# Neighbours' product with W_l made once per node: the mean layer of a graph network gathers products in place of rows

## The chip, the cores and the metric

The kernel runs as one program on one core of a Trainium2 chip. The metric is the device time of one execution in microseconds (us); of several runs the median is given. All arithmetic is float32 unless a type is named.

Names: PE is TensorE, which multiplies matrices; PEld are its weight loads; DVE is VectorE, ACT is ScalarE, POOL is GpSimd, which here issues the gathers and the scatter-adds (indirect DMAs); SP issues the plain DMAs. SBUF is the on-chip memory, PSUM the accumulators that PE writes.

## The reference

There are N = 3125 nodes with D = 512 features and E = 50000 edges (src, dst), sorted by dst. Four residual layers follow one another:

```
x = x + attention(layernorm(x))       # 8 heads, softmax over the edges into a node
x = x + ffn0(layernorm(x))            # 8 experts, each takes its best 256 nodes
x = x + mean(layernorm(x))            # below
x = x + ffn1(layernorm(x))            # 64 experts, 2 per node, and a shared dense part
...
def mean(x):                          # W_l, W_r: 512 x 512
    agg = segment_sum(x[src], dst)    # sum over the edges into a node
    h = (agg / max(deg, 1)) @ W_l + b + x @ W_r
    return h * sigmoid(h)
...
def ffn0(x):                          # expert e: W1[e] 512 x 128, W2[e] 128 x 512
    h = gelu(x[idx[e]] @ W1[e] + b1[e])
    out[idx[e]] += vals[e] * (h @ W2[e] + b2[e])
```

The sum over the edges and the product with W_l can change places: agg @ W_l = segment_sum((x @ W_l)[src], dst).

## The kernel before

Nodes are handled in NT = 25 tiles of 128 (the last has 53). The edges of a tile stand in 17 columns of 128 edges: 16 columns belong each to a quarter tile of 32 nodes (QCOLS = 4 columns for each of 4 quarters), and one column, gathered into the buffer sr, takes what does not fit. One gather (L121, an indirect DMA by POOL) brings one column: 128 rows of 512 features and a tail.

The stages follow one another. (1) A front prepares edge lists and the attention table. (2) The attention loop (gat_tiles) goes over the tiles: 17 gathers tgx a tile in groups of up to six columns; DVE weighs them (L882); PE adds them up per node by one-hot matrices (L899, messages). Beside it the class Rows makes, one tile later, what the first FFN needs: statistics and square root (stats, ACT L595), the normalised row (normal, stored to ec_table), its transposes in PSUM tile ec_tp (turn, copied by ACT L613), and router logits (logits, then take). Also beside it, the one-hot of the next tile is transposed (L826), copied by ACT (tohrt, L828) and multiplied into tpd (L836). (3) The class Choice finds each expert's 256 nodes by a serial chain of small DVE instructions and small PE sums. (4) The first FFN (expert_choice) goes over 8 experts: gather two halves of rows (ec_x), transposes, W1, GELU, W2, bias, gate, and a scatter-add into xd per half (L1266). The two halves name different rows and do not wait for each other; the next expert's wait for them. (5) Statistics of xd are computed and stored in its column D (the reciprocal deviation rs). (6) The mean and dense loop goes over the tiles as described next. (7) The experts' loop runs the 64 routed experts.

In stage 6 (second_half) edges(t) adds the 17 gathered columns, each weighed by the sender's rs, into a PSUM tile: first the column sr (L1823), then 32 matmul records for the 16 columns sx (L1829). DVE takes mean and variance of the sum (L1839 to L1841), ACT writes the mean row (L1843). PE transposes it (turned, L1849; ACT copies it out, L1851) and mean_layer multiplies: four products of mt with W_l and four of xt with W_r into one accumulator (product, L1859). DVE adds the bias (L1864), ACT applies SiLU (L1865), DVE adds the residual. The row is normalised; of it come the gate (L1877, read by DVE at L1381), the up products with two weights (read by ACT at L1884 and DVE at L1885) and the down product (DVE L1891).

The loop is software-pipelined by hand. PE's order in iteration i is: transposes of mean(i), xn2(i), xn3(i-1) and s(i-2); edges(i+1); mean_layer(i); gate(i-1); up(i-1); down(i-2). The instructions marked with pin stay in the written order on their engine. POOL's only work there is fetch(i+2): first sr, then 16 gathers into sx. sr has 2 buffers (se_r) and sx has 7 of four columns each (se_g), so a gather waits until the matmul that reads the older contents is done.

## Time and profile before

| what | time |
|---|---|
| median of 3 runs | 2334.58 us (2333.31 to 2347.64) |
| the profiled execution | 2344.47 us |
| its span | 2342.7 us, mean granted PE clock 0.833 |
| front | 0 to 196 us |
| attention loop | 196 to 850 us |
| choice of nodes | 850 to 945 us |
| first FFN | 945 to 1020 us |
| statistics | 1020 to 1050 us |
| mean and dense loop | 1050 to 1840 us |
| experts' loop | 1840 to 2342.7 us |

The limits of the stages are read from the timeline. The page's first part gives the busy time of each engine over the span:

```
PE 1639.1 (70%) x6698; PEld 804.5 (34%) x6698; DVE 1039.3 (44%) x2902; ACT 469.3 (20%) x876; POOL 1103.7 (47%) x1140
```

A row of the page's fifth part gives line, engine, operation, what is written and read with the shapes, the count; then the busy time of the group, the mean duration of one instruction in ns, and the idle time of that engine just before such an instruction, with what ended most of it. A float32 matmul stands in the records as more than one instruction: four products with a 512 x 512 weight are 8 records of 0.43 us at the full clock. An instruction that issues a DMA counts as busy only while it prepares it. "remote" as a releaser means that no event in the records names who ended the wait.

### The profile page before, as it was taken

The numbers are of one execution on the slowest core, as the hardware profiler recorded it, in microseconds if no ns is written. First come the engines' busy times: TensorE is split into PE (matmuls) and PEld (weight loads), VectorE is DVE, ScalarE is ACT, GpSimd is POOL, SyncE is SP. The second block draws the span as 40 slices with busy tenths as digits, with TensorE's granted clock in tenths as the row PEclk, the third lists the DMA queues.
The fourth block names the chain that finished last, engine by engine and source line by source line (L and its number), as shares of the span: only waits on it lengthen the run. The fifth ranks groups of instructions, "written<-read, shape, count | busy, mean of one in ns | idle before, by whom it ended". The sixth has DMA issues, their size and how long they took to land. (4 is left out here: it accounts for less than half of the span.)

```text
span 2342.7 us, 22566 instructions
## 1 busy us (share of the span) xinstructions
PE 1639.1 (70%) x6698; PEld 804.5 (34%) x6698; DVE 1039.3 (44%) x2902; ACT 469.3 (20%) x876; POOL 1103.7 (47%) x1140
## 2 busy tenths in 40 slices
PE   6683545554545532612799989989999899889986
PEld 3351222222222222400344444444444454445443
DVE  6354567666766757240233433433444422233221
ACT  1010112122222210100222222222223121112111
POOL 1404666666666600526555555555530245445443
PEclk9896666666766665855899999999999999999998
DMA  5115676776777653667666666666662499899981
GB/s 166 40 58 154 198 213 194 215 212 195 214 207 209 201 182 124 119 158 208 185 186 191 190 191 181 189 191 182 188 186 94 156 330 308 277 320 300 299 274 32
DMA packets 182468, 451.84 MB, mean 193 GB/s; under 512 B 48036, under 2 KB 51947, under 8 KB 182202
## 3 DMA queue, kind: packets, MB, share of 16 engines
q0 software_dynamic: 91840, 266.53, 42.1%
q1 hardware_dynamic: 79434, 182.03, 21.8%
q10 hardware_dynamic: 11056, 1.67, 0.4%
q8 instruction: 59, 0.97, 0.2%
q14 instruction: 79, 0.65, 0.1%
HBM read 399.52 MB, written 65.01 MB: 198 GB/s over the span
## 5 line engine op out<-in xcount | busy, mean ns | idle before, releaser
L121 POOL DMA_INDIRECT tgx<-gat_table,sidx x417 | 399.7, 958 | 220.4 <-issue 147.8
L121 POOL DMA_INDIRECT sx<-xd,sidx x392 | 372.0, 949 | 143.8 <-issue 113.6
L882 DVE TENSOR_TENSOR tgx<-tgx,aside 128x3072 f32<-128x3072 f32 (+2 forms) x74 | 233.5, 3157 | 58.9 <-ACT aside L876 45.6
L899 PE MATMUL tpm<-tgx,toh 128*32 128x256 f32 (+1 forms) x1568 | 200.4, 554 | 48.2 <-issue 38.6
L1859 PE MATMUL acc<-sh_w,x3t 128*128 128x512 f32 x400 | 177.1, 595 | 0.0
L1649 DVE TENSOR_TENSOR re_s<-re_s,re_ph 128x256 f32<-128x256 f32 x72 | 30.3, 421 | 267.0 <-ACT re_s L1648 263.8
L1646 PE MATMUL re_ph<-sx,re_xt 128*128 128x512 f32 x320 | 148.6, 608 | 0.0
L1653 POOL DMA_INDIRECT out<-re_y,re_both x32 | 50.3, 1572 | 181.2 <-DMA out<-re_y,re_others 151.4
L836 PE MATMUL tpd<-dpart,toht 128*128 128x192 bf16 x100 | 18.2, 329 | 158.3 <-ACT tohrt L828 138.3
L899 PEld LDWEIGHTS tpm<-tgx,toh 128*32 128x32 f32 x1568 | 68.5, 139 | 161.9 <-issue 125.8
L121 POOL DMA_INDIRECT re_x<-moe_table,node x64 | 64.7, 1011 | 120.1 <-DVE destf L1504 91.7
L1646 PE MATMUL re_ph<-w,re_xt 128*128 128x512 f32 x256 | 118.8, 608 | 0.0
L121 POOL DMA_INDIRECT sr<-xd,sidx x25 | 23.7, 947 | 191.1 <-PE acc L1823 156.8
L1829 PE MATMUL acc<-sx,qoh 128*32 128x512 f32 x784 | 97.0, 621 | 11.6 <-DVE qoh L1826 7.9
L1859 PEld LDWEIGHTS acc<-sh_w,x3t 128*128 128x128 f32 x400 | 74.2, 190 | 84.2 <-issue 84.2
L306 PE MATMUL pw<-gat_w,fr_xt 128*128 128x512 f32 x200 | 99.9, 647 | 1.7 <-issue 1.7
L1859 PE MATMUL acc<-sh_wl,mt 128*128 128x512 f32 x200 | 95.1, 619 | 2.9 <-issue 2.9
L899 PE MATMUL tpm<-tgx,tohr 128*128 128x256 f32 (+3 forms) x104 | 54.3, 637 | 54.3 <-issue 24.7
L1839 DVE BATCH_NORM_STATS2 e_st<-acc 128x6 f32<-128x512 f32 (+1 forms) x25 | 17.5, 699 | 167.3 <-PE acc L1829 121.1
L1859 PE MATMUL acc<-sh_w,sh_ht 128*128 128x512 f32 x200 | 90.2, 593 | 1.3 <-ACT sh_ht L1851 1.2
L1859 PE MATMUL acc<-sh_wr,xt 128*128 128x512 f32 x200 | 89.9, 592 | 0.0
L846 DVE TENSOR_REDUCE tdm<-tpd 128x128 f32<-128x384 f32 (+2 forms) x77 | 28.1, 421 | 126.8 <-PE tpd L838 87.7
(434 smaller groups left out, 2746.4 us busy)
## 6 DMA issues: line engine op xcount, KB each, us to landing
sx<-in_L_ffn_w SPq DMA_DIRECT2D x120, 512.0 KB
w<-in_L_ffn_w SPq DMA_DIRECT2D x64, 512.0 KB
wo<-in_L_ffn_w SPq DMA_DIRECT2D x32, 512.0 KB
tgx<-gat_table,sidx POOLq DMA_INDIRECT x417
gat_table<-row SPq DMA_DIRECT2D x24, 264.0 KB
xd<-xres SPq DMA_DIRECT2D x24, 264.0 KB
ec_table<-ec_row SPq DMA_DIRECT2D x24, 264.0 KB
sx<-xd,sidx POOLq DMA_INDIRECT x392
```

Of the source, the lines that this page charges most:

```text
L121: return nc.gpsimd.indirect_dma_start(out=out, out_offset=None, in_=table, in_offset=bass.IndirectOffsetOnAxis(ap=idx, axis=0),)
L306: pin(nc.tensor.matmul(pw, xts[t][:, k, :], w[:, k].rearrange("p h d -> p (h d)"), start=(k == 0), stop=(k == KD - 1)))
L836: pin(nc.tensor.matmul(pd[:, j // PDJ, j % PDJ * w:(j % PDJ + 1) * w], oht[:, j * P:(j + 1) * P], part4[:, t].rearrange("p i w -> p (i w)" ...
L846: pin(nc.vector.tensor_reduce(to, v.rearrange("p (c i h) -> p c h i", c=n, i=3), AX.X, OP.add))
L882: pin(nc.vector.tensor_mul(msg, msg, wgt[:, a:b, :, None].to_broadcast([P, g, H, DH])))
L899: pin(nc.tensor.matmul(pm[own, b, :cols.stop - cols.start], left, x[:, j, cols], **at))
L1646: self.pin(nc.tensor.matmul(ph, xt[:, k, :], w13[:, :, k, :], start=(k == 0), stop=(k == KD - 1)))
L1649: self.pin(nc.vector.tensor_mul(s, s, ph[:, 1]))
L1653: return self.nc.gpsimd.indirect_dma_start(out=self.out, out_offset=bass.IndirectOffsetOnAxis(ap=dest, axis=0), in_=y, in_offset=None, bou ...
L1829: pin(nc.tensor.matmul(pm[i * Q:(i + 1) * Q, :], oh[:, j, i, :], x[:, i, :D], start=False, stop=(j == QCOLS - 1)))
L1839: pin(nc.vector.bn_stats(st[:n], pm[:n]))
L1859: pin(nc.tensor.matmul(po, xt[:, i % KD, :], w[:, i % KD, :], start=(i == 0), stop=(i == n - 1)))
```

## The change

The attention loop makes V = xn @ W_l for each tile of nodes, from the transposes that the logits use already. ACT scales it back by the deviation (dev) and writes it to a buffer (given), and SP stores it to a new table vd. W_l is loaded early, and the mean of each of its columns is taken from it once (at t = 1), so that a row and the row less its mean give the same product. b2 W_l is formed once (t = 3 and 5).

Because the first FFN changes x after that, it adds its own share to vd: W2 W_l is formed per expert during the choice, as a list of 40 pieces (8 sets of four transposes, 32 products) of which a few are issued after each sum on PE (beside). Each expert then has two more products with W2 W_l, two more bias additions, and two more scatter-adds, into vd. The gate's scale moves from DVE to ACT.

The statistics store rs in vd's column D; xd loses its tail and its second half. In the mean loop the gathers read vd, so what is summed is already multiplied by W_l; the sum of edges goes straight into the accumulator of xn2 @ W_r. As xn2 is scaled by the degree first (rs2 multiplied by it), DVE multiplies the whole by 1/degree and adds the bias in one instruction. The mean's statistics, its row, its transposes and the product with W_l are gone. The loop is re-indexed: iteration i fetches for i+1 and sums the edges of i.

PE's order there becomes: transposes of xn2(i), xn3(i-1), s(i-2); xn2 @ W_r; the 16 columns sx; the column sr, which closes the sum; gate(i-1); up(i-1); down(i-2). sx has 8 buffers. The first three experts' weights are loaded in iteration 2 of this loop (before: beside the first FFN), the later five after the last mean layer.

```diff
--- before.py
+++ after.py
...
-EARLY, LATE = 3, 4
+EARLY, LATE = 3, 5
...
+        self.given = [sb.tile([P, XROW], F32, name=f"ec_given{i}", bufs=1) for i in range(2)]
...
-    def logits(self, t):
+        pin(nc.scalar.copy(self.xt, pt))
+    def logits(self, t, to):
+        self.lp = to
         for k in range(KD):
-            self.pin(self.nc.tensor.matmul(self.pt[:, 0, :X0], self.xt[:, k, :], self.wr[:, k, :],
+            self.pin(self.nc.tensor.matmul(to, self.xt[:, k, :], self.wr[:, k, :],
                                            start=(k == 0), stop=(k == KD - 1)))
+        self.pv = self.ps.tile([P, KD, P], F32, name="ec_tp").rearrange("p k w -> p (k w)")
+        for k in range(KD):
+            self.pin(self.nc.tensor.matmul(self.pv, self.xt[:, k, :], self.wl[:, k, :],
+                                           start=(k == 0), stop=(k == KD - 1)))
 
     def take(self, t):
-        self.pin(self.nc.vector.tensor_copy(self.lg[:, t, :], self.pt[:, 0, :X0]))
+        nc, pin = self.nc, self.pin
+        pin(nc.vector.tensor_copy(self.lg[:, t, :], self.lp))
+        v, n = self.given[t % 2], rows(t)
+        pin(nc.scalar.activation(v[:, :D], self.pv, AF.Copy, scale=self.dev.pop(t)))
+        nc.sync.dma_start(self.vd[t * P:t * P + n, :], v[:n])
+        if t == 1:
+            pc = self.ps.tile([P, KD, P], F32, name="ec_tp").rearrange("p k w -> p (k w)")
+            for k in range(KD):
+                pin(nc.tensor.matmul(pc, self.c["ones"], self.wl[:, k, :], start=(k == 0), stop=(k == KD - 1)))
+            pin(nc.vector.scalar_tensor_tensor(self.wl, pc[:, None, :].to_broadcast([P, KD, D]), -1.0 / D, self.wl,
+                                               op0=OP.mult, op1=OP.add))
+        if t == 3:
+            pb = self.ps.tile([P, KD, P], F32, name="ec_tp")
+            for k in range(KD):
+                pin(nc.tensor.transpose(pb[:, k, :X0], self.b2[:, k * P:(k + 1) * P], self.c["ident"][:X0, :X0]))
+            self.bt = self.sb.tile([P, KD, X0], F32, name="ec_bt", bufs=1)
+            pin(nc.vector.tensor_copy(self.bt, pb[:, :, :X0]))
+        if t == 5:
+            pb = self.ps.tile([P, KD, P], F32, name="ec_tp").rearrange("p k w -> p (k w)")
+            for k in range(KD):
+                pin(nc.tensor.matmul(pb[:X0], self.bt[:, k, :], self.wl[:, k, :], start=(k == 0), stop=(k == KD - 1)))
+            b = self.sb.tile([X0, D], F32, name="ec_bv", bufs=1)
+            pin(nc.vector.tensor_copy(b, pb[:X0]))
+            nc.sync.dma_start(self.b2d, b)
...
-                nodes.logits(t - 1)
+                nodes.logits(t - 1, logit)
...
+    def beside(self, n):
+        for _ in range(min(n, len(self.pieces))):
+            self.pieces.pop(0)()
...
             all_ = self.ps.tile([P, 3], F32, name="ch_ps")
             pin(nc.tensor.matmul(all_, self.k["same"], cnt, start=True, stop=True))
+            self.beside(1)
...
+            turned = {}
+            def turn2(e):
+                pt = ps.tile([P, KD, P], F32, name="w2_tp")
+                for i in range(KD):
+                    pin(nc.tensor.transpose(pt[:, i, :], w2[:, e, i * P:(i + 1) * P], c["ident"]))
+                turned[e] = ch.tile([P, KD, P], F32, name="w2_t", bufs=2)
+                pin(nc.scalar.copy(turned[e], pt))
+            def times_wl(e, i):
+                if i == 0:
+                    turned["to"] = ps.tile([P, D], F32, name="w2_ps")
+                to = turned["to"]
+                pin(nc.tensor.matmul(to, turned[e][:, i, :], wl[:, i, :], start=(i == 0), stop=(i == KD - 1)))
+                if i == KD - 1:
+                    pin(nc.scalar.copy(w2v[:, e], to))
+            pieces = [lambda: turn2(0)]
+            for e in range(X0):
+                if e + 1 < X0:
+                    pieces.append(lambda e=e: turn2(e + 1))
+                pieces += [lambda e=e, i=i: times_wl(e, i) for i in range(KD)]
+            choice = Choice(nc, pin, c, k, ch, ps, mine, pieces)
...
-                adds = []
+                for j, (w, b, to) in enumerate(((w2, b2t, xd), (w2v, b2v, vd))):
+                    adds = []
+                    for h in range(HALVES):
+                        py = ps.tile([P, D], F32, name=f"py{j}")
+                        pin(nc.tensor.matmul(py, ht[:, h * P:(h + 1) * P], w[:, e, :], start=True, stop=True))
+                        y = ys[j][(2 * e + h) % 4]
+                        pin(nc.vector.tensor_add(y[:, :D], py, b[:, e, :]))
+                        gate = x[e, h][:, D + e:D + e + 1]
+                        pin(nc.scalar.activation(y[:, :D], y[:, :D], AF.Copy, scale=gate))
+                        adds.append(nc.gpsimd.indirect_dma_start(
+                            out=to, out_offset=bass.IndirectOffsetOnAxis(ap=node[:, h * X0 + e:h * X0 + e + 1], axis=0),
+                            in_=y, in_offset=None, compute_op=OP.add,
+                        ))
+                    tc.declare_no_dep(adds[1].ins, adds[0].ins, reason="different rows of the table")
                 for h in range(HALVES):
-                    py = ps.tile([P, D], F32, name="py")
-                    pin(nc.tensor.matmul(py, ht[:, h * P:(h + 1) * P], w2[:, e, :], start=True, stop=True))
-                    y = ys[(2 * e + h) % 4]
-                    pin(nc.vector.tensor_add(y[:, :D], py, b2t[:, e, :]))
-                    gate = x.pop((e, h))[:, D + e:D + e + 1]
-                    pin(nc.vector.tensor_scalar(y[:, :D], y[:, :D], gate, None, op0=OP.mult))
-                    adds.append(nc.gpsimd.indirect_dma_start(
-                        out=xd[:N], out_offset=bass.IndirectOffsetOnAxis(ap=node[:, h * X0 + e:h * X0 + e + 1], axis=0),
-                        in_=y, in_offset=None, compute_op=OP.add,
-                    ))
-                tc.declare_no_dep(adds[1].ins, adds[0].ins, reason="different rows of the table")
+                    x.pop((e, h))
...
-                nc.scalar.dma_start(xd[g * P:(g + n) * P, D:D + 1].rearrange("(t p) o -> p t o", p=P), rs[:, :n, None])
+                nc.scalar.dma_start(vd[g * P:(g + n) * P, D:D + 1].rearrange("(t p) o -> p t o", p=P), rs[:, :n, None])
...
+        nc.vector.tensor_mul(rs2, rs2, rdeg[:, 1])
+        gp = ctx.enter_context(tc.tile_pool(name="se_g", bufs=8))
...
-                gather(nc, x[:, 0, :], xd[:N], sidx[:, c0:c0 + 1])
+                gather(nc, x[:, 0, :], vd, sidx[:, c0:c0 + 1])
                 xs = [x]
                 for j in range(QCOLS):
                     x = gp.tile([P, 4, XROW], F32, name="sx")
                     for i in range(m):
                         col = c0 + 1 + j * m + i
-                        gather(nc, x[:, i, :], xd[:N], sidx[:, col:col + 1])
+                        gather(nc, x[:, i, :], vd, sidx[:, col:col + 1])
                     xs.append(x)
...
-            def edges(t):
+            def edges(t, pm):
                 c0, m = tile_cols(t)[0], quarters(t)
                 oh, xs = state.pop(("oh", t)), state.pop(("sx", t))
-                pm = ps_a.tile([P, D], F32, name="acc")
                 ohr = wk.tile([P, P], F32, name="qohr", bufs=2)
                 pin(nc.vector.tensor_scalar(ohr, c["iota_f"][:, :P], sloc[:, c0:c0 + 1], xs[0][:, 0, D:D + 1],
                                             op0=OP.is_equal, op1=OP.mult))
-                pin(nc.tensor.matmul(pm[:m * Q], ohr[:, :m * Q], xs[0][:, 0, :D], start=True, stop=False))
                 for j in range(QCOLS):
-                    x = xs[1 + j]
                     pin(nc.vector.tensor_tensor(oh[:, j, :m], oh[:, j, :m],
-                                                x[:, :m, D:D + 1].to_broadcast([P, m, Q]), OP.mult))
+                                                xs[1 + j][:, :m, D:D + 1].to_broadcast([P, m, Q]), OP.mult))
                     for i in range(m):
-                        pin(nc.tensor.matmul(pm[i * Q:(i + 1) * Q, :], oh[:, j, i, :], x[:, i, :D],
-                                             start=False, stop=(j == QCOLS - 1)))
-                n = m
-                mean = wk.tile([P, D], F32, name="mean")
-                n = n * Q
-                if n < P:
-                    pin(nc.vector.memset(mean, 0.0))
-                st = wk.tile([P, 6], F32, name="e_st", bufs=2)
-                mv = wk.tile([P, 2], F32, name="e_mv", bufs=2)
-                shift = wk.tile([P, 1], F32, name="e_shift", bufs=2)
-                pin(nc.vector.bn_stats(st[:n], pm[:n]))
-                pin(nc.vector.bn_aggr(mv[:n], st[:n]))
-                pin(nc.vector.scalar_tensor_tensor(shift[:n], mv[:n, 0:1], -1.0, rdeg[:n, t:t + 1],
-                                                   op0=OP.mult, op1=OP.mult))
-                pin(nc.scalar.activation(mean[:n], pm[:n], AF.Identity, bias=shift[:n], scale=rdeg[:n, t:t + 1]))
-                state["mean", t] = mean
+                        pin(nc.tensor.matmul(pm[i * Q:(i + 1) * Q, :], oh[:, j, i, :], xs[1 + j][:, i, :D],
+                                             start=False, stop=False))
+                pin(nc.tensor.matmul(pm, ohr, xs[0][:, 0, :D], start=False, stop=True))
...
-            def mean_layer(t, mt, xt):
-                pw = product([(mt, wl), (xt, wr)])
-                pin(nc.vector.tensor_add(pw, pw, bias))
+            def mean_layer(t, xt):
+                pw = ps_a.tile([P, D], F32, name="acc")
+                for k in range(KD):
+                    pin(nc.tensor.matmul(pw, xt[:, k, :], wr[:, k, :], start=(k == 0), stop=False))
+                edges(t, pw)
+                pin(nc.vector.scalar_tensor_tensor(pw, pw, rdeg[:, 0, t:t + 1], bias, op0=OP.mult, op1=OP.add))
                 pin(nc.scalar.activation(pw, pw, AF.Silu))
...
             fetch(0)
             one_hot(0)
-            for i in range(-1, NT - 1):
+            load(1)
+            normal(0)
+            for i in range(NT - 1):
                 if i + 2 < NT:
                     load(i + 2)
-                    fetch(i + 2)
-                    one_hot(i + 2)
-                mt = xt = x3t = ht = None
-                if i >= 0:
-                    mt = turned(state.pop(("mean", i)), "mt")
-                    xt = turned(state.pop(("xn2", i)), "xt")
+                fetch(i + 1)
+                one_hot(i + 1)
+                if i == 2:
+                    early += [weights.load(e) for e in range(EARLY)]
+                x3t = ht = None
+                xt = turned(state.pop(("xn2", i)), "xt")
                 if i >= 1:
                     x3t = turned(state.pop(("xn3", i - 1)), "x3t")
                 if i >= 2:
                     ht = turned(state.pop(("s", i - 2)), "sh_ht")
-                edges(i + 1)
                 normal(i + 1)
                 chosen, pairs = todo.pop(("choose", i), None), todo.pop(("places", i), None)
                 if chosen:
                     chosen = router.choose(*chosen)
                 if pairs:
                     pairs = router.places(*pairs)
-                if i >= 0:
-                    mean_layer(i, mt, xt)
+                mean_layer(i, xt)
                 if i >= 1:
                     gate(i - 1, x3t)
                     up(i - 1, x3t)
...
-            weights.gp = gp
-            early += [weights.load(EARLY + k) for k in range(LATE)]
             t = NT - 1
             x, z = todo.pop(("choose", t))
             assert not todo and z == t - 1
-            mt = turned(state.pop(("mean", t)), "mt")
             xt = turned(state.pop(("xn2", t)), "xt")
             x3t = turned(state.pop(("xn3", t - 1)), "x3t")
             ht = turned(state.pop(("s", t - 2)), "sh_ht")
             first = router.choose(x, z)
-            mean_layer(t, mt, xt)
+            mean_layer(t, xt)
+            weights.gp = gp
+            early += [weights.load(EARLY + k) for k in range(LATE)]
```

## The prediction

> **What bounds the kernel now.** I read four views: the costliest groups of the page, the busy time cut at the stages, the timeline of one tile of the long loop, and the waits. The windows, cut at the ends of the attention loop (850), the choice (945), the first FFN (1020), the statistics (1050) and the loop over mean and dense layers (1840), say which engine could be the limit where; the columns are length, then busy time of PE, its weight loads, DVE, ACT, POOL, then granted clock, DMA share and GB/s:
>
> ```profile
> 196.00:850.00 654.00, 332.42 (x2122) 157.39 (x2122) 425.70 (x786) 136.83 (x297) 399.92 (x421) 0.66 0.69 200
> 850.00:945.00 95.00, 24.38 (x98) 19.43 (x99) 55.42 (x217) 4.31 (x6) 5.73 (x6) 0.50 0.53 181
> 945.00:1020.00 75.00, 41.82 (x147) 26.62 (x145) 18.64 (x32) 13.06 (x23) 35.48 (x26) 0.82 0.58 95
> 1050.00:1840.00 790.00, 662.17 (x2504) 301.25 (x2504) 300.70 (x973) 201.84 (x278) 396.16 (x419) 0.93 0.60 177
> ```
>
> The mean and dense loop is a third of the span, and PE is busy for 84% of it. That invites the reading "PE is the bound, take PE work away". The page's groups give the prices:
>
> ```profile
> L121 POOL DMA_INDIRECT tgx<-gat_table,sidx x417 | 399.7, 958 | 220.4 <-issue 147.8
> L121 POOL DMA_INDIRECT sr<-xd,sidx x25 | 23.7, 947 | 191.1 <-PE acc L1823 156.8
> L1859 PE MATMUL acc<-sh_wl,mt 128*128 128x512 f32 x200 | 95.1, 619 | 2.9 <-issue 2.9
> L1859 PE MATMUL acc<-sh_wr,xt 128*128 128x512 f32 x200 | 89.9, 592 | 0.0
> ```
>
> The second row is the one to stop at: POOL idles 157 us in front of the gather sr, because sr's two buffers come free by a matmul of the edges (L1823). So PE lets the stream of gathers start, once a tile. The timeline of one tile (start, length, what, in brackets the idle time before) shows what happens then:
>
> ```profile
> 1368.46 1.13 PE L1823 MATMUL acc<-sr,qohr 128*128 128x512 f32 x2 [0.55 <-DVE qohr L1821]
> 1369.52 3.64 PE L1829 MATMUL acc<-sx,qoh 128*32 128x512 f32 x32
> 1369.86 0.95 POOL L121 DMA_INDIRECT sr<-xd,sidx  x1 [7.42 <-PE acc L1823]
> 1371.11 0.94 POOL L121 DMA_INDIRECT sx<-xd,sidx  x1 [0.30 <-issue]
> ...
> 1380.06 1.00 PE L1877 MATMUL misc<-gt,x3t 128*128 128x64 f32 x8
> ...
> 1380.89 7.09 PE L1859 MATMUL acc<-sh_w,x3t 128*128 128x512 f32 x16
> ...
> 1387.82 3.60 PE L1859 MATMUL acc<-sh_w,sh_ht 128*128 128x512 f32 x8
> ...
> 1394.01 0.23 DVE L1381 COPY logit<-misc 128x64 f32<-128x64 f32 x1 [3.70 <-remote]
> 1394.11 0.60 ACT L1884 ACTIVATE sh_s<-acc 128x512 f32<-128x512 f32 x1 [4.18 <-remote]
> ...
> 1398.34 0.95 POOL L121 DMA_INDIRECT sr<-xd,sidx  x1 [7.54 <-PE acc L1823]
> ```
>
> The gate's matmuls (L1877) end at 1381.06, but their reader on DVE (L1381) starts at 1394.01. The first half of the up product ends at about 1384.5; its reader on ACT (L1884) starts at 1394.11. DVE and ACT had nothing left from 1390.3 and 1389.9. 17 gathers run from 1369.86 to 1390.79, one per 1.25 us, and their last bytes land at 1394.1 by the DMA records. In some 18 of the loop's tiles the same 13.0 and 9.6 us stand there. Completions that fall in the first 4 us of a stream are seen within 1 us (edges to L1839: 0.9), those with no gather in flight after 0.1. I read this as a rule of this trace: **deep in a stream of gathers, a product of PE is seen only when the stream has drained**. A tile is then stream 20.95, drain 3.2, and a chain of 4.3 to the next sr: 28.5 us. PE's 25 us fit inside; they are not what sets it. The waits of the attention loop look the same:
>
> ```profile
> ACT tohrt L828 <- remote: 168.1, 18, 14.5
> ```
>
> (sum, count, mean us of idle time.) That copy reads a transpose which had ended 9 us earlier where I looked (717.87 to 726.69), and restarts with POOL's next gather at 726.89.
>
> **The change, part by part.**
>
> *Mean loop, removed per tile:* four wl products (8 records, 3.7 us), four transposes and mt's copy, bn_stats, aggregate, shift on DVE (0.70, 0.18, 0.16) and the mean on ACT (0.78). PE falls from 25.3 to about 21.2 us (transposes 3 x 0.5, wr 3.6, edges 3.64, sr 1.1, gate 1.0, up 7.1, down 3.6), level with POOL's 17 gathers (21.3). None of this lies on the chain stream, drain, restart, so by itself it is worth nothing.
>
> *Moved:* edges now add into wr's accumulator. Order on PE before: mt, xt, x3t, ht transposes, sr's matmul, sx's 32, wl, wr. After: xt, x3t, ht transposes, wr, sx's 32, and sr's matmul last (it closes the sum). POOL's fetch still begins with sr and sr still has two buffers, so the stream that was let go by the first matmul of the edges is let go by the last, with wr ahead of it as well. The eighth sx buffer gives nothing, for sr stands ahead of it in the queue. With T0 the end of sr's matmul: stream from T0+0.35 to T0+21.3, drained at T0+24.5. After T0 PE has gate, up, down and the next xt and x3t transposes, 12.7 us, then ht's transposes, which need sh_s from the up product (ended at T0+4.6 and T0+8.1, so deep in the stream) and is held. From the drain: L1884 0.60, multiply 0.69, ht's transposes 0.66 with 0.2 of handing over, wr 3.6, sx matmuls 3.64, sr 1.1. Pitch = 24.5 + 10.5 = 35.0, against 28.5: **+6.5 per tile, 24 tiles, +156**.
>
> Here PE stands still from T0+12.7 to T0+26. The trace's row: in the attention loop, with such holes (9.1 us ahead of L836), the granted clock is 0.66, against 0.93 here with holes of 2.9. The Trainium skill ("TensorE: Matmul & The Clock Gate", section "What's actually happening") says that the array falls to half clock after an idle window of about 3.4 us and needs as long busy to come back. By the rule wr and the edges after each hole lose up to 3.4/2 to 3.4 us: +41 to +82. It speaks against the change, since less PE work makes longer holes. In the sum I leave it out, for half of the loop's matmuls here would still run back to back; the range has it.
>
> *Attention loop, added per tile:* V = xn W_l, 4 matmuls (8 records; 3.7 us at full clock, up to 7 at half), an ACT copy with a scale (0.6 to 0.8), a store of 264 KB; three one-off pieces (about 10 us in all, beside gathers). PE is busy 51% there, so the matmuls fit in. But ACT's copy of V waits for PE, and behind it in ACT's order stand the next tile's sqrt (L600, with a table load of 1.28) and tohrt's copy. If V is held to the drain as tohrt is, 0.7 + 1.3 + 0.3 = 2.3 us are put ahead of tohrt after it, and tpd, the reduce and the exponentials follow. Whether POOL's next stream waits for them: its buffers come free by earlier groups. Bounds 0 and +5 per tile (V at half clock ahead of group 0's messages besides), below nothing excluded, for nothing is taken away there. SP's tdst loads keep their place ahead of the new store. The nearest row is POOL's restart 0.2 us after tohrt, which is released at the same instant and not by it; I take +0.8 per tile: **+20** (0 to +120).
>
> *Choice:* 8 sets of transposes and 32 products of W2 with W_l in PE's gaps. At this stage's clock (0.50) about 1.3 and 1.75 each, 66 us; PE is idle for 70.6 of 95, so they just fit, in gaps that a serial DVE chain makes. Each can push a small matmul of that chain by at most 1.75, and some ten that remain at the end stand ahead of b1's transpose. **+8** (0 to +25).
>
> *First FFN:* two more products, adds and scatter-adds per expert. PE, DVE and ACT have room (42, 19, 13 of 75). POOL does not: a scatter-add is 1.59 us with 0.30 between. Per expert four of them and two gathers (0.98): 10.1 us, 81 for eight, with 11 of start and landing 92, against 75. Today's adds leave POOL waiting on each other's landing, which the new ones, to another table, can fill; that is in the 92. **+17** (0 to +35).
>
> *Other moves:* three experts' weights (4.5 MB) go from the first FFN's time to the third tile of the mean loop, where DMA is 60% busy, and the broadcast b2v adds 2 MB earlier: 0, covered by the DMA share; uncovered, some 5 us of drain in two tiles. The later sets are issued after the last mean layer: 0 (to +10); three sets are there. rs2 and deg: one small DVE multiply. Experts' loop: unchanged.
>
> Sum: 156 + 20 + 8 + 17 = +201. The profiled execution took 2344.5 (span 2342.7), 9.9 above the median of 2334.6, so on the median's scale 2535.
>
> **The rivals.**
>
> *Faster: completions are not what holds the tile.* If the late readers belong to before's order and the new one (few products between T0 and the stream's start) escapes, or the records mislead, the tile costs the larger of POOL's 21.3 and PE's 21.2 with today's 2.9 of waiting: 24.1, which is -4.4 x 24 = -106; with the +45 of the other stages -61: 2274. For it: the last tiles, without gathers in flight, run at 25 to 26.5, PE's own pace; wr is sometimes seen in time (L1864 3.1 us after its end). Against it: that 13.0 and 9.6 come back tile after tile, and in the attention loop too. It decides from the point where the up product's reader starts within about 4 us of its end.
>
> *Slower by the added work alone.* The held readers stay, but the chain after the drain is as short as now (wr running ahead before ht's transposes, or the stream starting with the edges): pitch 28.5 to 29.5, 0 to +24, with +45: 2370 to 2395.
>
> *The clock.* As forecast, with 3.4 us lost to half clock in each tile, or the attention loop at +5: 2535 + 60 or so, to 2600.
>
> **How the numbers follow.** Forecast (with its clock variant) 0.61, own range 2420 to 2600; added work alone 0.13; faster 0.26. About 1% is what a measurement here can tell from no change. Of the faster case 0.22 keeps more than 1% (it must lose no more than 38 us of its 61 to a dearer attention loop), 0.04 falls within 1%, with 0.02 more from a cheap version of the second rival; slower has the rest, 0.72. The range must take in half of the faster case to leave no more than 2 in 10 out: 2274 to 2600.
>
> **What would show it.** In the changed profile: idle time of sr on POOL (157) rises to 24 x about 13, or falls near nothing in the faster case; its releaser is the closing matmul of the edges; L1884's and the logit copy's counterparts start together at the drain; the windows of the loop show a clock well under 0.93 (forecast) or PE busy over 88% (faster). The attention loop's end is at 850 + 20, the first FFN has 32 scatter-adds and ends some 45 later. The forecast is wrong if the pitch of the mean loop is under 28.

## The result, and the profile after

The changed kernel takes 2485.1 us (median of 4 runs, 2479.1 to 2493.4), the kernel before beside it 2338.5: the ratio is 1.0625 (95% interval 1.0576 to 1.0674). It is slower by 6%. The profiled execution took 2479.1, its span is 2477.3.

Where the 134.6 us between the two profiled spans lie, with the stages cut at the same instructions in both (last message of the attention loop, first and last scatter-add, first matmul of the experts):

| stage | before | after | difference | forecast |
|---|---|---|---|---|
| to the end of the attention loop | 836.0 | 891.3 | +55.3 | +20 |
| choice of nodes | 113.8 | 133.9 | +20.1 | +8 |
| first FFN, its adds | 66.5 | 74.9 | +8.4 | +17 |
| statistics, mean and dense loop | 828.6 | 898.6 | +70.0 | +156 |
| experts | 497.8 | 478.6 | -19.2 | 0 |

The windows of the changed kernel, cut at its own stages (columns as in the prediction: attention loop, choice, first FFN, mean and dense loop):

```profile
196.00:891.00 695.00, 431.58 (x2302) 189.05 (x2302) 426.35 (x776) 148.39 (x316) 399.95 (x417) 0.73 0.66 195
891.00:1025.00 134.00, 91.03 (x252) 46.15 (x251) 60.30 (x232) 19.63 (x33) 5.98 (x10) 0.67 0.36 117
1025.00:1100.00 75.00, 49.49 (x163) 29.28 (x161) 20.83 (x32) 33.92 (x51) 60.20 (x42) 0.90 0.96 155
1165.00:1955.00 790.00, 561.20 (x2064) 250.38 (x2064) 243.54 (x759) 158.88 (x214) 375.77 (x396) 0.85 0.56 166
```

The last row ends with the last sums of edges; the prediction's window of before went on for 70 us behind them, so the two do not hold the same work. Over the whole stage (1100.1 to 1998.7 us, before 1016.3 to 1844.9) PE is busy for 607 us in place of 664, and the stage is 70 us longer: less work for PE did not make it shorter. The granted clock fell from 0.93 to 0.85 in the loop. The gathers of the mean loop before, which the prediction shows for sr alone, and then the groups of now:

```profile
L121 POOL DMA_INDIRECT sx<-xd,sidx x392 | 372.0, 949 | 143.8 <-issue 113.6
...
L121 POOL DMA_INDIRECT sx<-vd,sidx x392 | 372.1, 949 | 359.2 <-PE acc L1891 245.8
L121 POOL DMA_INDIRECT tgx<-gat_table,sidx x417 | 399.9, 959 | 266.0 <-issue 166.6
L1914 PE MATMUL acc<-sh_wr,xt 128*128 128x512 f32 x200 | 128.4, 801 | 0.8 <-issue 0.8
```

POOL's gathers are as long as before (949 and 959 ns). The idle time ahead of those into sx is now 359 us, and most of it ends with L1891, the sums of edges over sx; before, it was 144 us ahead of sx and 191 ahead of sr. It does not end with L1893, the closing matmul of sr. One tile of that loop, from the timeline:

```profile
1501.74 7.08 PE L1908 MATMUL acc<-sh_w,x3t 128*128 128x512 f32 x16
...
1505.79 0.60 ACT L1936 ACTIVATE sh_s<-acc 128x512 f32<-128x512 f32 x1
...
1508.66 3.60 PE L1908 MATMUL acc<-sh_w,sh_ht 128*128 128x512 f32 x8
...
1513.39 1.04 PE L1898 MATMUL tp<-ident,xn 128*128 128x128 f32 x8
...
1516.18 0.69 DVE L1943 TENSOR_TENSOR sh_o<-acc,x 128x512 f32<-128x512 f32 x1 [6.55 <-remote]
...
1517.82 0.95 POOL L121 DMA_INDIRECT sx<-vd,sidx  x1 [0.30 <-issue]
...
1521.88 0.59 ACT L1900 COPY xt<-tp 128x512 f32<-128x512 f32 x1 [15.50 <-remote]
...
1522.52 1.12 PE L1898 MATMUL tp<-ident,sh_s 128*128 128x128 f32 x4 [8.09 <-ACT xt L1900]
...
1523.43 4.83 PE L1914 MATMUL acc<-sh_wr,xt 128*128 128x512 f32 x8
...
1528.19 3.64 PE L1891 MATMUL acc<-sx,qoh 128*32 128x512 f32 x32
1529.64 0.94 POOL L121 DMA_INDIRECT sx<-vd,sidx  x1 [10.87 <-PE acc L1891]
```

The transposes of xn (L1898) end at 1514.43. ACT, which has nothing else to do, copies them at 1521.88; the last gather was issued at 1517.82 and its bytes landed at 1521.65. Then comes the chain: copy, ht's transposes (PE had stood still for 8.1 us), W_r, the sums, and POOL goes on at 1529.64 after 10.87 us. W_r takes 4.83 us here, 3.6 in the tiles of before: the clock has dropped in the hole (granted 1.00 from 1514.5 to 1519.0, 0.50 from 1519.1 to 1525.8, and 1.00 again from 1526.0).

### The profile page after: what moved, and what is told of

Same layout as the page of the kernel before. It is cut to its first block, busy times and chain, and to the rows that moved or that the text cites. A ratio compares the mean times of both kernels' runs of the same rounds, so it can differ in the third digit from the quotient of the medians.

```text
span 2477.3 us, 22626 instructions
## 1 busy us (share of the span) xinstructions
PE 1754.5 (71%) x6746; PEld 834.6 (34%) x6746; DVE 1020.8 (41%) x2829; ACT 485.4 (20%) x899; POOL 1128.7 (46%) x1157
## 5 line engine op out<-in xcount | busy, mean ns | idle before, releaser
L121 POOL DMA_INDIRECT sx<-vd,sidx x392 | 372.1, 949 | 359.2 <-PE acc L1891 245.8
L1718 PE MATMUL re_ph<-sx,re_xt 128*128 128x512 f32 x360 | 166.2, 605 | 0.0
L1891 PE MATMUL acc<-sx,qoh 128*32 128x512 f32 x784 | 110.5, 694 | 53.2 <-DVE qoh L1888 49.5
L1898 PE MATMUL tp<-ident,sh_s 128*128 128x128 f32 x100 | 25.4, 403 | 154.4 <-ACT xt L1900 135.9
L1914 PE MATMUL acc<-sh_wr,xt 128*128 128x512 f32 x200 | 128.4, 801 | 0.8 <-issue 0.8
L629 PE MATMUL ec_tp<-ec_wl,ec_xt 128*128 128x512 f32 x200 | 116.5, 733 | 1.2 <-issue 0.6
L883 DVE TENSOR_REDUCE tdm<-tpd 128x128 f32<-128x384 f32 (+2 forms) x77 | 28.1, 421 | 197.2 <-remote 72.6
L1916 DVE SCALAR_TENSOR_TENSOR acc<-acc,rdeg,sh_bias 128x512 f32<-128x512 f32 x25 | 19.0, 758 | 204.7 <-issue 97.7
L1718 PE MATMUL re_ph<-w,re_xt 128*128 128x512 f32 x216 | 99.8, 606 | 0.0
L1718 PEld LDWEIGHTS re_ph<-sx,re_xt 128*128 128x128 f32 x360 | 66.9, 196 | 67.3 <-issue 67.3
```

The lines of the kernel that those rows point to most:

```text
L121: return nc.gpsimd.indirect_dma_start(out=out, out_offset=None, in_=table, in_offset=bass.IndirectOffsetOnAxis(ap=idx, axis=0),)
L629: self.pin(self.nc.tensor.matmul(self.pv, self.xt[:, k, :], self.wl[:, k, :], start=(k == 0), stop=(k == KD - 1)))
L883: pin(nc.vector.tensor_reduce(to, v.rearrange("p (c i h) -> p c h i", c=n, i=3), AX.X, OP.add))
L1718: self.pin(nc.tensor.matmul(ph, xt[:, k, :], w13[:, :, k, :], start=(k == 0), stop=(k == KD - 1)))
L1891: pin(nc.tensor.matmul(pm[i * Q:(i + 1) * Q, :], oh[:, j, i, :], xs[1 + j][:, i, :D], start=False, stop=False))
L1914: pin(nc.tensor.matmul(pw, xt[:, k, :], wr[:, k, :], start=(k == 0), stop=False))
```

## The experiments

The experiments ran in later sessions than the first measurement, on three chips of one type (1, 4 and 11), and that turned out to matter. In each of these sessions the kernel before took 2126 to 2129 us, not 2335 to 2339. Which chip the first measurement ran on is not on record, so it is open whether the difference lies in the chip or in some condition of that session. Below they are called the first session and the later ones. Where an expectation speaks of a chip on which the kernel before takes 2335 us, it means the first session. Both kernels were run again unchanged, with a profile, beside experiments in one of the later sessions (chip 4).

**The two kernels again.**

> The kernel before, unchanged, for its profile beside the next three on the same chip. On the chip of the first four experiments the kernel before took 2129 us and not 2335. Theory (on that chip products are seen in time even deep in a stream of gathers, so the held chain is gone): where this run takes about 2130 us, the attention loop ends near 775 us and the distance of tiles in the mean loop is 25 to 26 us, PE's own pace; where it takes about 2335 us, the distance is 28.5 us and the readers of the gate and up products wait for the drain, as in the first profile.

> The changed kernel, unchanged, on the same chip. Theory for a chip where the kernel before takes 2130 us: the mean loop as in the run without products, 26 us a tile, attention and choice longer by some 9 and 19 us: 2195 to 2215 us, 3 to 4% slower than before. For a chip where the kernel before takes 2335 us: 2485 us as measured. Rival (the change costs the same everywhere): ratio 1.06 on both.

Measured: before 2127.3 in its profiled run (median of the runs beside it 2128.3), after 2204.9 (2200.5 to 2210.2), ratio 1.0345 (1.0296 to 1.0395). The windows of the attention loop and of the mean loop, the kernel before first:

```profile
196.00:719.00 523.00, 326.36 (x2072) 148.78 (x2072) 408.37 (x746) 136.08 (x285) 385.72 (x401) 0.68 0.81 238
...
941.00:1558.00 617.00, 582.14 (x2307) 262.97 (x2307) 260.14 (x803) 182.35 (x253) 392.70 (x413) 0.96 0.74 216
```

```profile
196.00:787.00 591.00, 403.43 (x2276) 179.06 (x2276) 413.13 (x750) 147.41 (x309) 383.30 (x401) 0.77 0.74 221
...
1063.00:1679.00 616.00, 536.75 (x2059) 233.04 (x2060) 244.86 (x758) 158.96 (x214) 379.81 (x396) 0.91 0.71 212
```

The attention loop of the kernel before ends at 718.7 (theory: 775) and its tiles are 21.6 us apart, 17 gathers of 1.25 us and nothing more; in the first session they were 25.4 apart. The mean loop's tiles are 25.5 us apart, and PE is busy for 94% of that loop. The readers of the transposes in the mean loop start within 0.1 us of the transposes or of the end of their engine's work, at any point of a stream. In the first session ACT's copy of xt started 3.3 to 8.8 us late in each of the 19 tiles of the changed kernel whose transposes ended 15 to 18 us into a stream. So the held readers (those that start late though their product is done and their engine is free) belong to the first session and not to the kernel. Here the change costs +68.6 in the attention loop, +15.7 in the choice, +11.1 in the FFN, -5.7 in the mean loop's stage and -9.6 in the experts. The waits of the changed kernel name two new causes (who waited for whom, then us in total, how often, the longest):

```profile
DVE tdm L883 <- PE tpd L625: 107.0, 23, 5.7
PEld acc L1891 <- DVE qoh L1888: 104.9, 37, 6.0
PE acc L1891 <- DVE qoh L1888: 77.8, 20, 5.2
POOL sx L121 <- PE acc L1891: 76.4, 16, 6.9
```

L883 are DVE's sums over tpd for the attention weights, L625 the router's logits, which the change moved into a free corner of tpd. L1888 scales the one-hots for the sums of edges.

**Sums of edges first.** The edit, in the mean loop (an excerpt, comments added):

```diff
...
+                edges(i)                 # starts the accumulator
                 xt = turned(state.pop(("xn2", i)), "xt")
...
                 mean_layer(i, xt)        # W_r closes it
+                prep(i + 1)              # DVE: qohr, qoh scaled by the deviation
...
```

> The sums of edges stand first in PE's order of each tile of the mean loop, ahead of the three sets of transposes; the product with W_r follows them and closes the sum; DVE's preparation of the one-hots is made one tile earlier. The work is the same. Theory (the tile is a stream of 17 gathers, its drain, and then the chain up to the first sums, which let the next stream go): nothing of the held chain is left ahead of the sums, so the distance of tiles falls from about 33 to 23 to 26 us, and the whole kernel from 2485 to 2270 to 2340 us. Rival (the loop is longer because PE, with longer holes, runs at a lower clock, or because the products in vd make the gathers slower): PE's and the gathers' work is unchanged, so 33 us and 2485 stay within 1%.

Measured 2130.2 us, ratio to before 1.0015 (1.0002 to 1.0028). Against the changed kernel's 1.0345 the gain is 75 us. The distance of tiles is 21.5 us, below what the theory said, since the gathers run without a break. No reader is held in that session, so it is not the held chain that this edit removed. It moves two things at once, PE's order and DVE's preparation; a later run tells them apart.

**W_r after the sums.** Only the order of the two in mean_layer is turned round; sr's matmul opens the sum.

> Only the product with W_r moves: after the transposes come the sums of edges and then W_r, in place of W_r and then the sums. Theory: the sums' start, which lets the stream go, comes earlier by the product's time, 3.6 to 4.8 us a tile, 24 tiles: 2485 falls by 85 to 115, to 2370 to 2400 us, and the idle time of POOL ahead of its gathers by as much. Rival (clock or gather speed): no change beyond 1%.

Measured 2265.3, ratio 1.065 (1.0621 to 1.0679): a miss, slower by 60 us than the changed kernel in a session of the same pace. The distance of tiles is 28.5, against 26.2. Here the sums wait for DVE's scaled one-hots, and W_r ahead of them filled part of that wait: PE's idle time ahead of the sums that ends with the one-hots is 124 us with W_r behind them, 78 with W_r ahead.

**Few gathers.**

```diff
...
-                    for i in range(m):
+                    for i in range(1):
...
                         gather(nc, x[:, i, :], vd, sidx[:, col:col + 1])
...
```

> Left out: three of every four gathers of the 16 columns in the mean loop; the sums read the gathered column four times, so PE, DVE and ACT work as before. 5 gathers in place of 17 make a stream of 6 us. Theory (products late in a stream are seen only when it has drained): no product is late any more, the distance of tiles falls to PE's own 21 to 23 us, the loop by some 240 us. Rival (the new order's chain or PE's clock sets the tile, and gathers only fill it): the distance stays above 29 us.

Measured: tiles 25.6 us apart, with 5 gathers, against 26.2 with 17, and not 21 to 23: the theory fails here, and the rival is right that the gathers only fill the tile (its 29 us was a figure of the first session). In every third tile it is 28 to 29 us, in the next 25 to 28, in the third 22.4, with or without the gathers. Something else in the new order sets them. Whether the loop of the first session would have become shorter was not tried.

**Without V and without the pieces.**

> Left out: the four matmuls of V in each tile of the attention loop (ACT scales the transposed row in V's place, the store to vd stays), and the 40 pieces that form W2 W_l beside the choice. Theory (V's matmuls come between the messages of a tile and what the next stream waits for): the attention loop ends at 836 to 845 us in place of 891, and the choice is 15 to 20 us shorter. Rival (it is the extra ACT copy ahead of the square root, or the stores, that cost): the attention loop still ends at 875 or later.

Measured (beside it the run with the sums of edges first, on the same chip, whose attention loop and choice are the changed kernel's): the loop ends at 777.9 against 786.6, the choice takes 115.8 against 135.1. So the pieces cost 19 us, as the theory said, but V's matmuls only 9, where the theory had some 50: there the rival holds. The stores and ACT's copy were still there, and so was the logits' place in tpd; the runs with the sums ahead of the logits, further down, tell these apart.

**W2 W_l in the loop of the first FFN, one expert ahead,** in place of the pieces, on top of the sums of edges first:

> The kernel with the sums of edges first, and W2 W_l of each expert formed in the loop of the first FFN, one expert ahead, in place of the 40 pieces beside the choice. Theory (the pieces make the choice about 19 us longer, since each stands ahead of a small matmul of the serial chain): the choice is 19 us shorter, the FFN at most 6 us longer, the whole 10 to 20 us below the same kernel with pieces (2130 us on the chip of the first four experiments). Rival (PE is as busy in the FFN as its adds allow): the FFN takes the 19 us instead.

Measured 2127.9, ratio to before 0.9993 (0.9975 to 1.0011), not distinguishable from the same kernel with pieces (1.0002 to 1.0028). Against the changed kernel in the same session the choice is 11 us shorter (123.2) and the FFN 7.5 longer (84.7): most of the time has moved and not gone, which is nearer to the rival.

**The sums over tpd ahead of the logits.** First on top of that kernel, then as the only edit of the changed kernel:

```diff
...
-            if t and a == col_groups(t)[-1][0]:
-                nodes.logits(t - 1, logit)
             if nxt and nxt[0] != t:
                 dm = collect(nxt[0])     # DVE: sums over tpd (comment added)
                 before, oh = pm, oh_next
+            if t and a == col_groups(t)[-1][0]:
+                nodes.logits(t - 1, logit)
...
```

> As the run before it, and in the attention loop DVE's sums over tpd for the next tile are issued ahead of the logits' matmuls, which since the change write a corner of the same PSUM tile. Theory (the sums wait for the logits only because both use tpd, 5.6 us a tile): the exponentials and the weighing start up to 5 us earlier in each tile, the attention loop's tile falls from 24.5 to 22 to 24 us, the whole by 10 to 50 us. Rival (the loop is set by the messages and the buffers): below 5 us.

> The changed kernel with one thing moved: in the attention loop DVE's sums over tpd for the next tile are issued ahead of the logits' matmuls. Theory: the attention loop alone gets back what it lost, 60 to 65 us where the kernel before takes 2130 us (2205 to about 2143), its tile at 21.6 us; the rest of the kernel unchanged. Rival (the gain in the earlier combination came from the two edits together): less than 30 us.

Measured 2058.8 (ratio 0.9667, 0.9617 to 0.9717), and alone 2143.1 (1.0066, 1.0041 to 1.0092). The edit leaves PE's order as it is; what changes is what DVE's sums wait for. Alone, the attention loop ends at 720.6 in place of 787.3: 67 of the 68.6 us are back, with V's matmuls, copy and stores all in place. Its window, and what is left of the wait:

```profile
196.00:721.00 525.00, 378.86 (x2280) 177.86 (x2280) 412.29 (x750) 149.89 (x309) 384.36 (x400) 0.79 0.82 249
```

```profile
DVE tdm L883 <- PE tpd L875: 1.8, 2, 1.4
```

The sums read columns 0 to 383 of each half of tpd, and 384 to 431 of the first. The logits stand in columns 504 to 511 of the first half, so no number is shared. Issued behind the logits, the sums waited for them all the same.

**Only DVE's preparation earlier.** PE's order is that of the changed kernel; prep(i + 1) stands after mean_layer(i), as in the first experiment.

> The changed kernel with one thing moved: DVE's preparation of the one-hots for the sums of edges (the instructions that scale them by the sender's deviation) is issued one tile earlier, after the mean layer's first DVE instruction. PE's order stays that of the changed kernel: transposes, W_r, sums. Theory (where products are seen in time, two tiles in three of the mean loop wait for this preparation, which stands behind the router's choice or other DVE work): where the kernel before takes 2130 us, the distance falls from 26.2 to about 22.5 us, the whole from 2205 by 75 to 95 us; where it takes 2335 us, only the tiles with a choice gain, 5 us each, 2485 falls by some 40. Rival (it is PE's order, W_r ahead of the sums, that costs): less than 20 us on either.

Measured 2120.9, ratio 0.9963 (0.9951 to 0.9974): 84 us below the changed kernel, and as good as the sums first. Tiles are 21.6 us apart. PE's order was not what cost. The wait in the changed kernel, in its timeline of the later session, and then what is left of it in the edited kernel (77.8 us before the edit):

```profile
1428.56 3.60 PE L1914 MATMUL acc<-sh_wr,xt 128*128 128x512 f32 x8
...
1436.64 0.34 DVE L1885 TENSOR_SCALAR qohr<-iota_f,sloc,sr 128x128 f32<-128x128 f32 x1
1436.89 0.89 DVE L1888 TENSOR_TENSOR qoh<-qoh,sx 128x128 f32<-128x128 f32 x4
1437.23 6.20 PE L1891 MATMUL acc<-sx,qoh 128*32 128x512 f32 x32 [5.08 <-DVE qoh L1888]
1439.55 0.94 POOL L121 DMA_INDIRECT sx<-vd,sidx  x1 [6.11 <-PE acc L1891]
```

```profile
PE acc L1895 <- DVE qoh L1886: 11.5, 5, 3.2
```

In a tile with a choice DVE works through the router's choice (from 1428.6 to 1436.7) before it comes to L1885; PE has finished W_r at 1432.2 and stands for 5.1 us, and POOL for 6.1 behind it.

**Both moves together.**

> The changed kernel with the two moves of the last two experiments together and nothing else: DVE's preparation one tile earlier in the mean loop, and DVE's sums over tpd ahead of the logits' matmuls in the attention loop. Theory (two separate waits of DVE's order, in two stages): the gains add up, 84 + 62 from 2205, so about 2059 us where the kernel before takes 2129, 3% faster than before. Rival (with both stages at the pace of the gathers, something shared, as the DMA queues, takes part of it back): 2090 us or more.

> The kernel of the last experiment once more, for whichever chip it meets. Where the kernel before takes about 2130 us: 2050 us again, ratio 0.96. Where it takes about 2335 us, and products deep in a stream of gathers are seen only at the drain: the attention loop and the tiles with a choice gain (45 and 40 us), the other tiles keep the held chain, so about 2400 us, still slower than before (theory); or the earlier preparation and sums free both loops there too, and it is faster than before (rival).

Measured 2051.8 (ratio 0.9635, 0.9606 to 0.9665) and 2054.9 (0.9659, 0.9614 to 0.9703). The gains add up, and the whole is 3.5% faster than the kernel before, with the change's own work in it. The kernel before was not given such moves. By its trace it has little room for them: its attention loop is at the gathers' 21.6 us a tile already, and PE is busy for 94% of its mean loop. Both runs met the same chip (4), and none met the conditions of the first session. Windows of its attention loop and of a stretch of its mean loop:

```profile
196.00:725.00 529.00, 378.08 (x2280) 176.97 (x2280) 412.12 (x750) 150.22 (x310) 384.12 (x401) 0.80 0.81 248
1000.00:1500.00 500.00, 477.58 (x1967) 217.52 (x1969) 238.32 (x720) 150.38 (x203) 375.46 (x395) 0.98 0.83 249
```

PE is busy 96% and POOL issues a gather every 1.25 us: the mean loop stands at both of its bounds together, at 21.6 us a tile where before has 25.5.

## Why the prediction was right, and which steps were not

The sign was right, and so was the stage with the largest loss: the mean loop's stage gives 70 of the 134.6 us. 2485 lies 50 below the forecast of 2535 and inside its own range. That the sum came so near is in part luck: the mean loop was forecast 86 us too dear, the attention loop and the choice together 47 us too cheap. By its steps:

*What bounds the mean loop.* That a reader late in a stream of gathers is held, and that the stream is PE's to let go, was seen again in the changed kernel, in the first session alone: the copy of xt at 1521.88 in the fence above. The products with W_l (95 us) are gone and the stage is longer, so less work for PE did not shorten it by itself. The rule as written, that a product is seen only at the drain, is too strong. In the same fence L1943 reads its product at 1516.18, 3.9 us after its end and 5.5 us ahead of the last landing. In the later sessions the faster rival's starting point holds (readers in time), and yet the changed kernel is slower there too, for reasons that neither case named.

*The chain in a tile.* The forecast had the up product held and ht's transposes behind it. That step failed: its reader L1936 starts at 1505.79, 0.4 us after the first half of the product and as soon as ACT has loaded its table. In most tiles of the changed kernel it is so, with first halves that end 7 to 10 us into a stream; the second halves end 11 to 13 us into it, and most of them are read after 0.1 us. The forecast let depth in the stream decide, yet in the kernel before the gate's product, 11.2 us into its stream, was not seen until the drain. So depth alone does not tell which product is held. What is held instead is ACT's copy of xt, whose transposes end 16.6 us into the stream. From the last landing to the start of W_r this other chain takes 1.8 us where the forecast had 2.2, so the error hardly shows in the number: luck again.

*The pitch of 35.0.* Measured 34.0 over 15 tiles in the middle, against 28.9, so +5.1 and not +6.5 a tile. Two more terms were wrong and nearly cancelled. "POOL's fetch still begins with sr": in the order that was built sr stands behind five or six gathers of sx. The first sx gather waits only for the first of the four sx blocks, so the stream is let go 1.4 us into the sums in place of at their end, 3.6 us earlier (sr's matmul ends at 1532.89, POOL went on at 1529.64 and not 0.35 after that). That gives 31.4. W_r behind the hole takes 1.2 us more than the 3.6 of the forecast, and the tiles without a choice measure 30.7 to 34. The tiles with a choice measure 37: the sums wait there for DVE's one-hots behind the router's choice, which the prediction passed over, since in the kernel before the sums stood ahead of the choice in DVE's order too.

*+156 for the stage.* Measured +70. The 24 distances add up to 789 us after and 713.6 before: +75, not 24 x 5.1, because the kernel before starts its loop slowly (57, 17 and 38 us for the first three). Re-indexing the loop costs 26 us ahead of the first sum and gives back 31 behind the last. The prediction took every tile at the steady difference.

*The clock.* In the tile above the granted clock falls to 0.50 some 4.6 us after PE's last matmul (1514.43) and is back at 1.00 some 3.4 us after PE goes on (1522.52). The Trainium skill's rule ("TensorE: Matmul & The Clock Gate", section "What's actually happening"), half clock after an idle window of about 3.4 us and as long busy to come back, agrees with that. From it the prediction worked out +41 to +82 and left them out of the sum. They should have gone in: W_r's group rose from 89.9 to 128.4 us, 38 us that lie on the chain. The sums' group rose from 97.0 to 110.5, but most of a tile's sums come after the stream has been let go.

*+20 in the attention loop.* Measured +55, and +69 in the later session. The step that failed is its mechanism: "ACT's copy of V waits for PE, and behind it in ACT's order stand the next tile's sqrt (L600, with a table load of 1.28) and tohrt's copy". V, its copy and its stores together leave about 2 us (720.6 against 718.7) in the later sessions once the sums over tpd are issued first. The cost is the move of the logits into tpd, which the diff shows in two lines and to which the prediction gave no price. For the first session this is argued and not shown, since the edit was not run there. Its rows of these sums, before and after, point the same way, since the idle time ahead of them rises by 70 us:

```profile
L846 DVE TENSOR_REDUCE tdm<-tpd 128x128 f32<-128x384 f32 (+2 forms) x77 | 28.1, 421 | 126.8 <-PE tpd L838 87.7
...
L883 DVE TENSOR_REDUCE tdm<-tpd 128x128 f32<-128x384 f32 (+2 forms) x77 | 28.1, 421 | 197.2 <-remote 72.6
```

*Choice +8, FFN +17.* Measured +20 and +8. Of the choice, 19 are the pieces by the run without them. The prediction took most of the 1.75 us of a product as hidden in PE's gaps; in this serial chain of small matmuls it is not. In the FFN POOL sets the length, as forecast: in the 75 us of its window 42 instructions of POOL are busy for 60.2 us, with 0.30 between them. Of the sixteen gathers that the forecast put into its sum, six stand ahead of the first scatter-add.

*Experts, 0.* Measured -19 and -10. The change loads eight sets of weights ahead in place of seven, and issues the later ones after the last mean layer; which of these it is was not tried.

Two slips in the working did no harm. The third figure of a wait is the longest and not the mean: for tohrt, 168.1 us in 18 times make a mean of 9.3, not 14.5. And the second rival should read 2380 to 2404 us, by the same scale as the forecast.

What stays open is why products are seen late in a stream in the first session and not in the others, and whether the two moves repair the changed kernel under its conditions: no experiment met them.

## What to carry to other kernels

When a change frees an engine, look at what lets the next stage of work start, and at the order on every engine ahead of it: in the later sessions two small groups of DVE instructions that stood behind something unrelated cost 84 and 62 us and hid a gain of 3.5%. A result put into a free corner of another result's tile is ordered with it, so ask who reads that tile next and in which order the two are issued. A bound read off one trace may belong to that chip or that session: profile the kernel before again beside the first experiment, before arguing from it.

## What the runs showed of the hardware

The same kernel took 2335 to 2339 us in the first session and 2126 to 2129 in all later ones, on three chips: 9% less. The gathers themselves were equally fast (949 to 960 ns to issue). Nearly the whole difference lies in the two loops with gathers in flight: the attention loop ends at 836 and at 718.7 us, and the tiles of the mean loop are 28.9 and 25.5 us apart. The place where it shows is between the end of a product on PE and the start of its reader. In the kernel before, in the first session, the gate's and the up product's readers start 13.0 and 9.6 us after the product in tile after tile, in most of them with their engines idle ahead of them. In the later session they start 3.3 to 7.0 and 0.4 to 4.2 us after it, and their engines have worked up to that moment. In the changed kernel of the first session, the halves of the up product, which end 7 to 13 us into a stream, are read within 0.4 us in most tiles, and xt's transposes, which end 15 to 18 us into it, 3.3 to 8.8 us late.
